# Gathers of two steps issued in one stretch, behind the messages of an odd step

## Chip, core and metric

The kernel runs on one core of a Trainium2 chip. A core has five engines with a queue each: PE (TensorE, matmuls), DVE (VectorE), ACT (ScalarE), POOL (GpSimd) and SP (SyncE, here only for issuing transfers). Each engine takes its instructions in the order of the program and waits on semaphores for the others. The metric is the device time of one execution in microseconds (us).

## What is computed

One layer of a graph network: 6250 nodes with 64 features, 206250 edges sorted by destination, four heads of 16.

```python
Qh = (x @ Wq.T + bq).reshape(n, H, D)
Kh = (x @ Wk.T + bk).reshape(n, H, D)
Vh = (x @ Wv.T + bv).reshape(n, H, D)
Ee = (edge_attr @ We.T + be).reshape(-1, H, D)
score = (Kh[src] * Qh[dst] * (1.0 / np.sqrt(D)) * Ee).sum(-1)
score = jnp.exp(jnp.clip(score, -5.0, 5.0))
msg = Vh[src] * score[..., None]
wV = jax.ops.segment_sum(msg, dst, num_segments=n)
x = _layernorm(x + wV.reshape(n, H * D), axis=-1)
```

## The kernel before

**Node stage.** K and V of all nodes go to a table `kv_tab` in DRAM, one row of 128 numbers a node, and Q to another. While PE computes the pieces of Q (L362, read by ACT at L364), POOL already gathers the rows of the first steps.

**Edge loop.** The edges are cut into 1612 tiles of 128. Eight tiles are a group, and the loop runs over 202 groups; a step is two groups (16 tiles), except for the last eight steps, of one group each. There are 105 steps. Each edge of a tile needs the K and V row of its source node. They come into one of five buffers `kvs[s % KVB]` (KVB = 5), one buffer a step, in two ways:

- 14 of a step's 16 tiles by POOL: `gather_kv` (L446) is one indirect DMA for one tile, 128 rows of 512 bytes. All edges of a tile are gathered at once.
- The last two tiles of steps 3 to 96 by PE: `hots` (L504, DVE) makes one-hot matrices in pieces, `picks` (L515 and L520) multiplies them with the nodes' features, `picked` (L527, L528, ACT) copies the result, `picked_kv` (L531 to L536) makes K and V of it in the PSUM bank `room`, and `place_kv` (L542, ACT) copies them into the buffer. A cycle of picks spreads over four groups, that is two steps, and has a `place_kv` in its second and in its fourth group.

Around it, for each group: `edges` (L561, PE) and `biased` (L567, ACT) make the edge values, `queries` (L573, PE) and `terms` (L580, DVE) multiply them with Q, `turn` (L585, PE) turns the product, `products` (L614 to L619, DVE) multiplies with K and sums to scores, `weigh` (L623, ACT) takes the exponential, and `message` (L630, DVE) multiplies V with it. For each step, `onehot_edges` (L606, DVE) and `widen` (L638, ACT) make a matrix of destinations, `sums` (L643, PE) adds the messages up in `room`, and `add` (L657, DVE) puts them onto the rows of the result. `sums`, `picked_kv`, `place_kv` and `add` share the bank `room`, so they take turns.

**Order.** The order on each engine is the program's. The message of a group is computed in the pass of the next group: in the pass of group g stands `message(g - 1)`. The message of a step's second group is the last reader of that step's buffer. In the pass of a step's first group, behind `message(g - 1)`, the program issues the gathers of the step KVB - 1 = 4 further on, into the buffer that the step before has just left. Each gather waits only for the readers of its own tile: those of the buffer's first eight tiles for the message of the first group, the others for that of the second. Since POOL does nothing else in the loop, its gathers run as far ahead as these waits allow. The products of a step wait for its gathers.

Of the kernel before, what the change touches and what calls it, by code (L numbers as in the profile page):

```python
# [25 lines left out]
NS = len(STEPS)  # L26
# [12 lines left out]
KVB = 5  # L39
# [9 lines left out]
def tiles_of(g):  # L49
    return min(G, T - g * G)  # L50
# [6 lines left out]
def groups_of(s):  # L57
    return range(STEPS[s][0], STEPS[s][0] + STEPS[s][1])
# [18 lines left out]
def picks_in(s):  # L77
    return 0 <= s < 2 * LAST


def is_picked(g, j):

    s = max(s for s in range(NS) if STEPS[s][0] <= g)
    return picks_in(s - AHEAD) and g == groups_of(s)[-1] and j >= G - 2
# [23 lines left out]
def tile_gnn(ctx: ExitStack, tc: tile.TileContext, x, xT, wT, bias, beT, weT, eT, src, src_rows, dst,  # L108
# [17 lines left out]
    def kv_of(g):  # L126

        s = max(s for s in range(NS) if STEPS[s][0] <= g)
        j = (g - STEPS[s][0]) * G
        return kvs[s % KVB][:, j:j + G, :]  # L130
# [39 lines left out]
    def fetch_edges(q):  # L170

        lo, hi = q * LG * G // 2, min((q + 1) * LG * G, T) // 2
        et = loads.tile([P, LG * G // 2, P], F32, name="et")
        nc.sync.dma_start(et[:, :hi - lo, :], eT[:, lo:hi, :])
        for g in range(q * LG, min((q + 1) * LG, NG)):
            ET[g] = et[:, (g % LG) * G // 2:(g % LG + 1) * G // 2, :]

    def fetch_queries(g):

        if g % RG == 0:  # L180
            for i in range(2):
                _, vs = nc.values_load_multi_w_load_instructions(
                    base[i:i + 1, g // 2:(g + RG) // 2], engines=[mybir.EngineType.SP], min_val=0,
                    max_val=N, skip_runtime_bounds_check_because="the least of some destinations")
                for k, v in enumerate(vs):
                    at[g + 2 * k + i] = v
        QW[g] = windows.tile([3 * W, C], BF16, name="qw")
        nc.sync.dma_start(QW[g], q3_tab[bass.ds(at[g], W), :].rearrange("n (i c) -> (n i) c", i=3))

    with tc.tile_pool(name="nodes", bufs=1) as nodes, \  # L190
# [22 lines left out]
        for i in range(NB // CB):  # L213
            s = slice(i * CB * P, (i + 1) * CB * P)
# [229 lines left out]
    def gather_kv(g, j):  # L444
        t = g * G + j
        nc.gpsimd.indirect_dma_start(  # L446
            out=kv_of(g)[:, j, :], out_offset=None, in_=kv_tab[:, :],
            in_offset=bass.IndirectOffsetOnAxis(ap=src_i[:, t:t + 1], axis=0))
# [8 lines left out]
    with tc.If(rv == 0) as branch:  # L457

        with tc.tile_pool(name="work", bufs=2) as work, \
# [21 lines left out]
            def pairs(ap):  # L481

                return ap.rearrange("p (a b) -> p a b", b=2)

            def fetch_sources(m):

                if m < LAST:
                    SRC[m] = work.tile([P, BATCH * P], I32, name="srcs")
                    nc.sync.dma_start(SRC[m], src_rows[m:m + 1, :].to_broadcast([P, BATCH * P]))
# [6 lines left out]
            def pieces(g):  # L496

                return [(g // 4, c) for c in PIECES[g % 4]] if 0 <= g < 4 * LAST else []

            def hots(m, c):  # L500
                lo, hi = CUTS[c], CUTS[c + 1]
                HOT[m, c] = work.tile([P, MOST, BATCH * P], BF16, name="hot", bufs=7)
                shape = [P, hi - lo, BATCH * P // 2, 2]
                nc.vector.tensor_tensor(  # L504
                    HOT[m, c][:, :hi - lo].rearrange("p b (a c) -> p b a c", c=2),
                    pairs(FROM[m])[:, None].to_broadcast(shape),
                    block2[:, lo:hi, None, :].to_broadcast(shape), op=OP.is_equal)
# [33 lines left out]
                n = tiles_in(to)  # L541
                nc.scalar.activation(kvs[to % KVB][:, n - 2:n, :], rooms, AF.Copy)  # L542

            def gather(s):

                for g in groups_of(s):
                    for j in range(tiles_of(g)):
                        if not is_picked(g, j):
                            gather_kv(g, j)

            def fetch_keys(g):

                n = tiles_of(g) * P
                KB[g] = work.tile([3 * W, G * P], BF16, name="kb", bufs=4)
                nc.sync.dma_start(KB[g][:, :n], key_tab[g // 2:g // 2 + 1, g % 2 * G * P:][:, :n]
                                  .to_broadcast([3 * W, n]))
# [54 lines left out]
            def products(g):  # L611
                n = tiles_of(g)
                prod = work.tile([P, G, C], F32, name="prod", bufs=1)
                nc.vector.tensor_mul(prod[:, :n, :], kv_of(g)[:, :n, :C], qe[g % 2][:, :n, :])  # L614
                SCORE[g] = work.tile([P, G, H], F32, name="score", bufs=3)
                score = SCORE[g][:, :n]
                nc.vector.tensor_reduce(score, prod[:, :n, :].rearrange("p g (h d) -> p g h d", h=H),  # L617
                                        axis=AX.X, op=OP.add)
                nc.vector.tensor_scalar(score, score, -5.0, 5.0, op0=OP.max, op1=OP.min)  # L619
# [80 lines left out]
            step_of = {g: s for s in range(NS) for g in groups_of(s)}  # L700
# [18 lines left out]
            biased(2)  # L719
            for mc in pieces(0):  # L720
                hots(*mc)
            for g in range(NG + 1):
                now, before = g < NG, g > 0
                i, m = g % 4, g // 4
                todo, ahead = pieces(g), pieces(g + 1)
                if g % LG == 0 and g + 3 * LG < NG:
                    fetch_edges(g // LG + 3)
                if i == 0 and m:
                    fetch_sources(m + 1)
                if g + 4 < NG:  # L730
                    fetch_queries(g + 4)
                if g + 6 < NG:
                    fetch_keys(g + 6)
                done = ends.get(g - 3)
                if now:
                    products(g)
                for mc in ahead[:1]:
                    hots(*mc)
                if done is not None:
                    add(done)  # L740
                if i == 0 and 0 < m <= LAST:
                    picked(m - 1)
                if i:
                    picks(todo)
                if g + 3 < NG:
                    edges(g + 3)
                if i == 0 and 4 <= g <= 4 * LAST + 2:
                    picked_kv(0)
                if g + 1 < NG:
                    turn(g + 1)  # L750
                if g + 2 < NG:
                    queries(g + 2)
                if g - 2 in ends:
                    sums(ends[g - 2])
                if i == 2 and 4 <= g <= 4 * LAST + 2:
                    picked_kv(1)
                if i == 0:
                    picks(todo)
                if g + 4 < NG:
                    onehot_rows(g + 4)  # L760
                    onehot_rows_rest(g + 4)
                if now:
                    weigh(g)
                else:
                    add(NS - 2)
                if g - 1 in ends:
                    widen(ends[g - 1])
                if g + 3 < NG:
                    biased(g + 3)
                if i == 2 and g < 4 * LAST:  # L770
                    sources(m + 1)
                if i in (1, 3) and 4 <= g <= 4 * LAST + 3:
                    place_kv(m - 1, i // 2)
                if before:
                    message(g - 1)
                if now and g == groups_of(step_of[g])[0] and step_of[g] + KVB - 1 < NS:
                    gather(step_of[g] + KVB - 1)
                if g in ends:
                    s = ends[g]
                    t0 = STEPS[s][0] * G  # L780
                    for t in range(t0, t0 + tiles_in(s)):
                        if t and t % KEYS == 0:
                            keys(t)
                    onehot_edges(s)
                for mc in ahead[1:]:
                    hots(*mc)
                if g + 2 < NG:
                    terms(g + 2)
                if done is not None:

                    while closed < B - 2 and due[closed] <= done + 1:
                        close(closed)
                        spreads(closed)
                        closed += 1
                    if closed in BATCHES and closed > scaled:
                        roots(scaled, closed)
                        scales(scaled, closed)
                        scaled = closed
                    for _ in range(3):
                        if normed < scaled:  # L800
                            norm(normed)
                            normed += 1
# [182 lines left out]
```

## Time and profile before

| | before |
|---|---|
| time, median of 3 runs | 2431.86 us (2424.51 to 2442.23) |
| the profiled execution: time | 2424.42 us |
| the profiled execution: span, mean granted PE clock | 2422.5 us, 0.858 |
| busy: PE, DVE, POOL, ACT | 1953.4, 1479.8, 1352.1, 931.0 us |
| DMA, software queue (the gathers) | 92.37 MB, 14.7% of 16 engines' span |
| DMA, hardware queue (all other) | 133.27 MB, 18.4% |

The span runs from the first to the last instruction of the profiled execution. A line of the timeline gives start and length in us, engine, line of the program, operation, what it writes and reads, and in brackets how long the engine was idle before it and what ended that. "Remote" there is a release that the profile can't put down to an instruction, "issue" one for which it shows no wait. Ends of matmuls are modelled, so an engine that waits for PE can tell more of PE's end than PE's own line. The granted clock is the share of its full clock that PE was given.

### The profile page before, as it was taken

The page shows a single profiled execution, that of the slowest core. Times are in us where ns is not written, and L with a number is a line of the kernel's source. Part 1 is how long each engine was busy: PE and PEld are TensorE (multiplying, and loading weights), DVE is VectorE, ACT ScalarE, POOL GpSimd, SP SyncE. Part 2 cuts the span into 40 slices and gives each one's busy share as a digit, 9 for nine tenths or more (in the row PEclk, how much of TensorE's full clock was granted, in tenths as well). Part 3 has the DMA queues.
Part 4 walks back from the last instruction along what each step waited for, and adds up shares of the span by engine and source line. Part 5 has one row for each costly group of instructions (what it writes and reads, how often), then busy time and mean ns, then how long its engine had stood idle before and what let it go on. Part 6 is the DMA issues. An engine that isn't in the chain of part 4 may idle for free.

```text
span 2422.5 us, 29177 instructions
## 1 busy us (share of the span) xinstructions
PE 1953.4 (81%) x10687; PEld 1157.5 (48%) x10687; DVE 1479.8 (61%) x2314; ACT 931.0 (38%) x1270; POOL 1352.1 (56%) x1434
## 2 busy tenths in 40 slices
PE   4468788788788798888788789788888788878876
PEld 4434444445445455445445445444545445545554
DVE  2356666666666666666666566666666666756654
ACT  1244334344344334424344343343443443443452
POOL 5426555555556565655656555655655655655552
PEclk9998888888889889888888888888879878878975
DMA  4423333233333333333333233333333333332331
GB/s 113 136 78 100 89 95 99 83 102 99 84 102 101 90 97 97 106 86 96 88 101 100 84 100 88 94 102 81 104 104 86 101 102 82 100 98 84 91 103 28
DMA packets 140879, 228.59 MB, mean 94 GB/s; under 512 B 71142, under 2 KB 71592, under 8 KB 140614
## 3 DMA queue, kind: packets, MB, share of 16 engines
q1 hardware_dynamic: 94774, 133.27, 18.4%
q0 software_dynamic: 45568, 92.37, 14.7%
q8 instruction: 86, 1.41, 0.2%
q10 hardware_dynamic: 384, 1.00, 0.2%
q14 instruction: 67, 0.55, 0.1%
HBM read 218.71 MB, written 7.79 MB: 94 GB/s over the span
## 4 chain that ended last, share of the span: by engine, by line
PE 61%; another core or an unknown queue 19%; DVE 8%; ACT 6%; issue 6%; DMA 0%; POOL 0%; DVEq 0%; SPq 0%; ACTq 0%; POOLq 0%
PE pick L515 19%; PE room L643 11%; PE low L520 10%; PE ee L561 7%; PE qe L585 4%; DVE hot L504 3%; PE room L534 3%; PE qq L573 3%; PE room L536 2%; ACT to L598 1%; ACT off L638 1%; ACT eb L567 1%; ACT to L592 1%; PE room L531 1%
## 5 line engine op out<-in xcount | busy, mean ns | idle before, releaser
L446 POOL DMA_INDIRECT kv<-kv_tab,src_i x1392 | 1320.7, 949 | 1017.7 <-DVE msg L630 584.4
L504 DVE TENSOR_TENSOR hot<-from,still 128x2048 bf16<-128x2048 bf16 (+1 forms) x611 | 697.1, 1173 | 113.3 <-PE low L520 92.9
L515 PE MATMUL pick<-hot,parts 128*128 128x512 bf16 x2350 | 567.1, 392 | 7.4 <-issue 6.1
L643 PE MATMUL room<-msg,off 128*128 128x64 f32 x3224 | 440.6, 288 | 133.5 <-issue 127.1
L643 PEld LDWEIGHTS room<-msg,off 128*128 128x128 f32 x3224 | 412.8, 204 | 161.6 <-issue 153.3
L515 PEld LDWEIGHTS <-parts 128*128 128x128 bf16 x2350 | 228.3, 101 | 301.7 <-issue 84.8
L580 DVE TENSOR_TENSOR term<-eb,qq 128x512 f32<-128x512 f32 x202 | 138.2, 684 | 327.2 <-remote 183.9
L561 PE MATMUL ee<-et,we_sb 128*128 128x512 f32 x404 | 268.6, 736 | 80.3 <-issue 50.4
L542 ACT ACTIVATE kv<-room 128x256 f32<-128x256 f32 x94 | 36.0, 383 | 770.4 <-remote 362.2
L567 ACT ACTIVATE eb<-ee,be_col 128x512 f32<-128x512 f32 x202 | 136.3, 675 | 502.7 <-PE ee L561 224.0
L520 PE MATMUL low<-hot,parts 128*64 128x512 bf16 x2350 | 292.8, 384 | 0.6 <-issue 0.4
L657 DVE SCALAR_TENSOR_TENSOR acc<-room,above,acc 128x64 f32<-128x64 f32 x103 | 29.2, 283 | 374.0 <-ACT kv L542 336.6
L598 ACT ACTIVATE to<-to,one_p 126x1024 bf16<-126x1024 bf16 x202 | 231.5, 1146 | 6.6
L592 ACT ACTIVATE to<-kb,minus_row 126x1024 bf16<-126x1024 bf16 x202 | 230.3, 1140 | 0.8 <-DMA kb<-key_tab 0.8
L638 ACT ACTIVATE off<-of 128x2048 f32<-128x2048 bf16 (+2 forms) x105 | 191.8, 1827 | 45.7 <-PE room L643 24.2
L520 PEld LDWEIGHTS <-parts 128*64 128x64 bf16 x2350 | 117.6, 110 | 165.9 <-issue 86.7
L585 PEld LDWEIGHTS qe<-ident,term 128*128 128x128 f32 x806 | 121.7, 166 | 88.7 <-issue 72.1
L531 PE MATMUL room<-bkv_p,ones_b 3*128 3x256 bf16 x94 | 31.4, 334 | 156.3 <-DVE acc L657 152.1
L585 PE MATMUL qe<-ident,term 128*128 128x128 f32 x806 | 147.6, 315 | 4.5 <-DVE term L580 4.5
L561 PEld LDWEIGHTS ee<-et,we_sb 128*128 128x128 f32 x404 | 71.7, 212 | 154.6 <-issue 114.2
L617 DVE TENSOR_REDUCE score<-prod 128x32 f32<-128x512 f32 x202 | 138.3, 685 | 7.0
L614 DVE TENSOR_TENSOR prod<-kv,qe 128x512 f32<-128x512 f32 x202 | 137.5, 681 | 3.8 <-issue 0.2
(122 smaller groups left out, 1274.3 us busy)
## 6 DMA issues: line engine op xcount, KB each, us to landing
et<-in_eT SPq DMA_DIRECT2D x100, 512.0 KB
kb<-key_tab SPq DMA_DIRECT2D x201, 252.0 KB
kv<-kv_tab,src_i POOLq DMA_INDIRECT x1392
srcs<-in_src_rows SPq DMA_DIRECT2D x47, 256.0 KB
qw<-q_tab SPq DMA_DIRECT2D x202, 15.8 KB
kv_tab<-kv_sb SPq DMA_DIRECT2D x5, 640.0 KB
q_tab<-q SPq DMA_DIRECT2D x5, 480.0 KB
acc<-in_x SPq DMA_DIRECT2D x48, 32.0 KB
```

Of the source, the lines that this page charges most:

```text
L446: nc.gpsimd.indirect_dma_start(out=kv_of(g)[:, j, :], out_offset=None, in_=kv_tab[:, :], in_offset=bass.IndirectOffsetOnAxis(ap=src_i[:, t ...
L504: nc.vector.tensor_tensor(HOT[m, c][:, :hi - lo].rearrange("p b (a c) -> p b a c", c=2), pairs(FROM[m])[:, None].to_broadcast(shape), bloc ...
L515: nc.tensor.matmul(hi_mid, parts_flat[:, at:at + 2 * C], hot, start=b == 0, stop=b == NB - 1)
L520: nc.tensor.matmul(low[u * C:(u + 1) * C], parts_flat[:, at:at + C], hot, start=b < 2, stop=b >= NB - 2, skip_group_check=True)
L561: nc.tensor.matmul(ee[:, :n, :], we_sb, ET[g][:, :n, :], start=True, stop=True)
L567: nc.scalar.activation(EB[g][:, :n], ee[:, :n], AF.Identity, bias=be_col)
L585: nc.tensor.transpose(qe[g % 2][:, 2 * u:2 * u + 2, :].rearrange("p j c -> p (j c)"), TERM[g][:, u, :], ident)
L592: nc.scalar.activation(TO[g][:, :n, :], KB.pop(g)[:, :n * P].rearrange("p (j e) -> p j e", j=n), AF.Square, bias=minus_row3[:3 * W])
L598: nc.scalar.activation(TO[g][:, :n, :], TO[g][:, :n, :], AF.Relu, bias=one_p[:3 * W], scale=-1.0)
L617: nc.vector.tensor_reduce(score, prod[:, :n, :].rearrange("p g (h d) -> p g h d", h=H), axis=AX.X, op=OP.add)
L638: nc.scalar.activation(OF[s][:, :n, :], OH.pop(s)[:, :n, :], AF.Copy)
L643: nc.tensor.matmul(pa, OF[s][:, j, :], MSG[s][:, j, :], start=j == 0, stop=j == n - 1)
```

## The change

The gathers of step 4 are issued once ahead of the loop. In the loop, the gathers are issued only in the pass of the first group of an even step s (from step 2 on), for the two steps s + 3 and s + 4 together, behind the message of the last group of the odd step s - 1. The last tile to be gathered of step s + 4 comes first, then all tiles of step s + 3, then the other tiles of step s + 4. Step s + 3 goes into the buffer of step s - 2, step s + 4 into that of step s - 1. The number of gathers and everything on the other engines stay as they are.

```diff
-            def gather(s):
-
-                for g in groups_of(s):
-                    for j in range(tiles_of(g)):
-                        if not is_picked(g, j):
-                            gather_kv(g, j)
+            def tiles_to_gather(s):
+
+                return [(g, j) for g in groups_of(s) for j in range(tiles_of(g)) if not is_picked(g, j)] \
+                    if s < NS else []
+
+            def gathers(s):
+
+                first, then = tiles_to_gather(s), tiles_to_gather(s + 1)
+                for g, j in then[-1:] + first + then[:-1]:
+                    gather_kv(g, j)
...
             for mc in pieces(0):
                 hots(*mc)
+            for g, j in tiles_to_gather(KVB - 1):
+                gather_kv(g, j)
             for g in range(NG + 1):
...
                 if before:
                     message(g - 1)
-                if now and g == groups_of(step_of[g])[0] and step_of[g] + KVB - 1 < NS:
-                    gather(step_of[g] + KVB - 1)
+                if now and g == groups_of(step_of[g])[0] and step_of[g] % 2 == 0 and g:
+                    gathers(step_of[g] + KVB - 2)
```

## The prediction, made before the changed kernel ran

> **What bounds the kernel now.** I read the page first: PE is busy for 81% of the span, POOL for 56%, and the chain that ended last is 61% PE with 19% put down to "another core or an unknown queue". One core runs, so that second share is time the chain could not explain. POOL issues nothing but gathers in the loop:
>
> ```profile
> L446 POOL DMA_INDIRECT kv<-kv_tab,src_i x1392 | 1320.7, 949 | 1017.7 <-DVE msg L630 584.4
> ```
>
> By this line POOL waits 584.4 us for messages, which is the idle time that the change reduces. Idle time matters only where somebody needs the gathers, so next I read the list of waits for who waits in the loop:
>
> ```profile
> POOL kv L446 <- DVE msg L630: 584.4, 139, 38.5
> ...
> ACT kv L542 <- remote: 362.2, 39, 13.2
> DVE acc L657 <- ACT kv L542: 336.6, 80, 7.4
> ```
>
> No VectorE product is listed as waiting for a gather. What stands out is ACT at L542 (`place_kv`), which holds up the add (L657), PE behind it (L531), and the message and POOL behind those. So I read two steps in the middle, PE's busy time window by window (columns: length, then busy us of PE, PEld, DVE, ACT, POOL, granted clock, DMA share, GB/s):
>
> ```profile
> 1166.00:1201.00 35.00, 34.13 (x205) 20.04 (x205) 25.40 (x37) 16.94 (x22) 21.07 (x23) 0.93 0.38 110
> 1201.00:1211.70 10.70, 4.03 (x12) 1.89 (x11) 4.09 (x9) 1.58 (x4) 5.63 (x6) 0.69 0.17 44
> 1211.70:1248.40 36.70, 36.27 (x214) 21.21 (x214) 26.66 (x38) 16.80 (x21) 22.55 (x24) 0.95 0.38 108
> 1248.40:1257.20 8.80, 0.00 (x0) 0.00 (x0) 2.22 (x6) 0.87 (x3) 4.13 (x5) 0.55 0.14 40
> ```
>
> Two steps take 45.6 us (POOL's 14-gather runs start at 1190.70 and 1236.31). PE is full for some 36.5 us of it and then stands nearly still for 9. The timeline of all engines shows what ends that stall:
>
> ```profile
> 1236.31 0.94 POOL L446 DMA_INDIRECT kv<-kv_tab,src_i  x1 [3.42 <-DVE msg L630]
> ...
> 1247.70 0.67 PE L561 MATMUL ee<-et,we_sb 128*128 128x512 f32 x1 [0.16 <-issue]
> ...
> 1252.81 0.94 POOL L446 DMA_INDIRECT kv<-kv_tab,src_i  x1 [0.30 <-issue]
> 1256.33 0.38 ACT L542 ACTIVATE kv<-room 128x256 f32<-128x256 f32 x1 [11.54 <-remote]
> ```
>
> PE's last matmul ends on record at 1248.4. `place_kv` waits for a PE semaphore and gets it at 1256.33, just after a run of 14 gathers, 20.0 us from the run's start: 1.43 us a gather, though POOL issues one each 1.25. I call run length times 1.43 the run's drain. It fits the shorter runs too: six gathers from 1258.09 (drain 1266.7; VectorE's hot, waiting for PE, starts 1266.57), eight from 1268.66 (drain 1280.1; `place_kv` 1280.18).
>
> Is that the gathers, or just PE's work? In one place the order slipped, so that only six gathers stood between two `place_kv`s:
>
> ```profile
> 957.60 0.38 ACT L542 ACTIVATE kv<-room 128x256 f32<-128x256 f32 x1 [7.84 <-remote]
> ...
> 970.63 0.38 ACT L542 ACTIVATE kv<-room 128x256 f32<-128x256 f32 x1 [1.46 <-PE room L643]
> ```
>
> The same half of the period takes 13.0 us there, and 21.8 with 14 gathers in it (1234.55 to 1256.33). So 8.8 us per two steps is the gathers' doing. The nearest row to what the change makes is in the node stage, where 30 gathers stand together while PE feeds ACT with q, one piece each 0.85 us:
>
> ```profile
> 65.47 0.94 POOL L446 DMA_INDIRECT kv<-kv_tab,src_i  x1 [22.85 <-DMA src_i<-in_src]
> ...
> 101.66 0.94 POOL L446 DMA_INDIRECT kv<-kv_tab,src_i  x1 [0.30 <-issue]
> ```
>
> ```profile
> 67.92 0.28 ACT L364 ACTIVATE q<-ps 128x128 bf16<-128x128 f32 x1 [0.41 <-issue]
> ...
> 82.45 0.28 ACT L364 ACTIVATE q<-ps 128x128 bf16<-128x128 f32 x1 [4.00 <-remote]
> 89.44 0.28 ACT L364 ACTIVATE q<-ps 128x128 bf16<-128x128 f32 x1 [6.71 <-remote]
> ...
> 99.24 0.28 ACT L364 ACTIVATE q<-ps 128x128 bf16<-128x128 f32 x1 [9.36 <-remote]
> ...
> 107.69 0.28 ACT L364 ACTIVATE q<-ps 128x128 bf16<-128x128 f32 x1 [1.00 <-remote]
> ```
>
> ```profile
> 50.00:65.00 15.00, 14.39 (x69) 14.14 (x67) 5.13 (x23) 6.66 (x22) 0.00 (x0) 1.00 0.58 218
> 66.00:108.00 42.00, 13.01 (x57) 12.21 (x56) 6.15 (x26) 5.80 (x26) 27.76 (x30) 1.00 0.41 124
> ```
>
> For the first 4 us nothing is lost. Then PE's word comes later and later (4, 7, 9 us apart) until 42.2 us after the first gather (1.41 each), when the rhythm is back. PE is busy for 13.0 of 42 us, at the full granted clock, against 14.4 of 15 before. Every record but PE's own completions stays punctual (DVE follows ACT at once). What is held up inside the chip the trace doesn't say; that it deepens with the run's length is what I use.
>
> **The change part by part.** *Waits removed.* Per two steps POOL stops three times now (runs of 14, 6, 8), and would stop once: message L630 of the odd step's last group releases the last tile of the later step, and the other 27 gathers need nothing later. The 27 are queued behind that wait; their readers are the products six and eight groups on. Six groups are 69 us at 11.4 us a group, the drain of 28 is 28 x 1.43 = 40 us, so no product waits: cost 0, and the saved idle is worth nothing by itself. The earlier step loses two groups of its lead of eight; cover 69 - 40 = 29 us.
>
> *The instructions.* 1392 gathers before and after, each 0.95 us on POOL; SP, ACT and PE queues keep their order. Step 4's 14 gathers already run at 121.2, ahead of the loop: 0.
>
> *The run.* Even steps 2 to 92 issue 28 gathers in one run: 46 runs. How much PE work fits beside one? PE busy in the 14-gather windows was 16.0 of 22 us (1189 to 1211) and 13.0 of 22 (1235 to 1257), in the 30-gather run 13.0 of 42, in the tail's 20-gather run (2355 to 2384) 16.6 of 29 at clock 0.68. It hardly grows with length, so for 28 I take 13 to 16.6, in the middle 14.8. Two steps need 36.5. The run starts 1.8 us after `place_kv` (1256.33 to 1258.09), as now. Period: 1.8 + 40 + (36.5 - 1.8 - 14.8 = 19.9) = 61.7, against 45.6: +16.1, times 46 = 741 us. From both ends: 18 us of work beside the run gives 58.5 (+593), 10 gives 66.5 (+961).
>
> *The stretch behind the drain* has 19.9 us of PE work and no gather. The granted clock was 0.51 from 1249 to 1263 and 1.00 from 1263 to 1281, so a cold start is already inside the 36.5. The Trainium skill (TensorE: Matmul & The Clock Gate, Part 1) has PE fall to half clock after an idle window of about 3.4 us and need as much activity to return; the 0.51 agrees. By that rule each longer stall could add an estimated 1.7 us, 78 us in all (3250); the sum below does without it.
>
> *The tail.* Runs of 8 and a last one of 20 become 16, 16, 16, 12. A longer run loses more, but the 20 goes away: between -14 (the 20-run held three groups for 28.7 us, 2355.1 to 2383.8, where free ones take 4.9 each, as from 2398.7 to 2413.3) and +26 (three 16-runs at the 8.8 of a 14-run). I take 0.
>
> Sum against the profiled execution (2424.4; the shown median is 7 higher): 2424 + 741 = 3165, and with the 7 about **3170 us**.
>
> **The rivals.** *1, faster.* The stall would be order, not starvation: `place_kv` simply lines up with the end of a run because the next run waits for it. Then one wait instead of three leaves POOL's 40.0 us plus one stop of 1.8 as the period: 41.8, -3.8 x 46 = -175, 2255 us. For it: POOL's work with its stops does fill 45.6 (40.0 + 1.8 + 1.8 + about 2). Against it: the 30-gather run, where POOL waits for nobody and ACT still gets PE's word 9 us apart. It decides if PE does its 36.5 us beside a 40 us run; it needs over 34 there and did 13. The Trainium skill (SBUF — State Buffer, Who interferes with whom) says that PE and ACT never wait on anyone and that only VectorE and GpSimd share a port; it speaks for this rival, and PE's 0.00 us busy from 1248.4 to 1257.2 speaks against it.
>
> *2, no change.* Each gather costs PE the same wherever it stands: 45.6 stays, 2430 us. Against it: 8.8 us lost to 14 gathers where six lost nothing.
>
> *3, slower, but less.* A 28-run loses only twice what a 14-run does: 36.5 + 17.6 = 54.1, +8.5 x 46 = 391, 2820 us. For it: the main loop's PE work (picks of 14 matmuls at a time) asks for fewer signals than the q stage. Against it: 13.0 of 42.
>
> *That the run breaks*, since gathers of the earlier step find a wait of their own, falls under 2; the releasing messages lie four groups back, so I see none.
>
> **How the numbers follow.** Forecast: 0.75; its own range is 3010 (2431 + 593 - 14) to 3420 (2431 + 961 + 26). Rival 3: 0.08. Rival 1: 0.13. Rival 2: 0.04. The range runs from 2750, which takes in rival 3, to 3420; it leaves out rivals 1 and 2 (0.17) and little above. About 1% is what this measurement can tell from no change. Faster 0.13, same 0.03 (most of rival 2), slower 0.84.
>
> **What would show it.** POOL: runs of 28, one wait for L630 per two steps, some 50 waits instead of 139. ACT's L542: the wait ahead of the drain grows from 8-13 to some 20 us. PE: windows of over 15 us almost empty in each period, then about 20 us full; granted clock below 0.858. Period near 62 us. I am wrong if PE stays busy through a run's second half, or if a product waits for a gather.

## The result, and the profile after

| four runs each | before | after |
|---|---|---|
| median | 2432.16 us (2424.51 to 2442.23) | 3218.43 us (3214.84 to 3222.48) |
| span of the profiled execution, granted clock | 2422.5 us, 0.858 | 3216.5 us, 0.770 |
| PE busy | 1953.4 us (81%) | 2058.0 us (64%) |
| ratio | | 1.323, 95% interval 1.318 to 1.328 |

The changed kernel is a third slower. The record names no chip for this comparison; its two kernels are taken as run on one. From L543 on its lines lie four further down than before's (L567 is now L571, L580 is L584, L630 is L634). The costliest group of POOL on the page after:

```profile
L446 POOL DMA_INDIRECT kv<-kv_tab,src_i x1392 | 1317.8, 947 | 1812.5 <-DVE msg L634 1359.7
```

The list of waits after (us in total, times, longest):

```profile
POOL kv L446 <- DVE msg L634: 1359.7, 49, 57.5
ACT eb L571 <- remote: 1328.4, 43, 35.1
DVE term L584 <- remote: 1078.3, 43, 29.3
...
PE room L647 <- issue: 918.3, 725, 3.2
...
ACT kv L542 <- remote: 76.7, 5, 16.5
```

POOL stops 49 times instead of 139, so the gathers do stand together. It waits 775 us more for messages all the same: they come late, because everything does. The waits that the profile can't put down to an instruction have moved: `place_kv` (L542) had 362.2 us of them and has 76.7, while `biased` on ACT and `terms` on DVE now have 43 each, some 31 and 25 us long. Both read what PE makes. PE itself stands ahead of its matmuls of `sums` (L647) for 918.3 us in 725 pieces, 127.1 in 165 before, and the profile shows nothing that it waits for there ("issue").

One period of the loop, window by window (length, then busy us of PE, PEld, DVE, ACT, POOL, granted clock, DMA share, GB/s). The run of 28 gathers starts at 1948.53:

```profile
1948.50:1958.50 10.00, 10.00 (x64) 4.60 (x62) 8.26 (x13) 6.62 (x8) 7.56 (x8) 1.00 0.61 183
1958.50:1968.50 10.00, 4.23 (x17) 2.07 (x13) 1.77 (x2) 0.00 (x0) 7.54 (x8) 0.84 0.22 54
1968.50:1978.50 10.00, 1.32 (x5) 1.72 (x6) 0.00 (x0) 0.00 (x0) 7.55 (x8) 0.50 0.21 52
1978.50:1988.20 9.70, 2.00 (x7) 1.65 (x7) 0.00 (x0) 0.04 (x1) 3.77 (x4) 0.50 0.14 34
1988.20:2007.10 18.90, 18.90 (x92) 10.42 (x93) 13.90 (x20) 9.42 (x12) 0.00 (x0) 0.79 0.19 57
```

For 10 us PE is full, for 30 it hardly works, and when the run is over it is full again. The timeline of the same stretch:

```profile
1948.53 0.94 POOL L446 DMA_INDIRECT kv<-kv_tab,src_i  x1 [27.81 <-DVE msg L634]
...
1978.89 0.26 PE L647 MATMUL room<-msg,off 128*128 128x64 f32 x1 [1.84 <-issue]
1980.99 0.27 PE L647 MATMUL room<-msg,off 128*128 128x64 f32 x1 [1.84 <-issue]
1983.79 0.26 PE L647 MATMUL room<-msg,off 128*128 128x64 f32 x1 [2.53 <-issue]
1985.19 0.26 PE L647 MATMUL room<-msg,off 128*128 128x64 f32 x1 [1.14 <-issue]
...
1988.16 0.69 ACT L571 ACTIVATE eb<-ee,be_col 128x512 f32<-128x512 f32 x1 [32.98 <-remote]
1988.33 0.69 DVE L584 TENSOR_TENSOR term<-eb,qq 128x512 f32<-128x512 f32 x1 [25.77 <-remote]
```

Two things are to be seen. PE's matmuls in the stall start 2.10, 2.80 and 1.40 us apart, multiples of 0.70: over the whole execution, 270, 192 and 171 gaps between starts lie at 0.64 to 0.76, 1.35 to 1.46 and 2.05 to 2.15 us. And ACT gets PE's word at 1988.16, 39.6 us from the run's start, or 1.415 us a gather: the 1.43 that the prediction took from before. In 40 of the 45 intervals between runs of 28 ACT's longest wait ends 39.4 to 39.9 us behind the run's first gather; in the other five ACT is released once in between, and again after 39.8 to 39.9 us.

### The profile page after: what moved, and what is told of

It reads as the page before. It is cut to its first block, busy times and chain, and to the rows that moved or that the text cites. A ratio compares the mean times of both kernels' runs of the same rounds, so it can differ in the third digit from the quotient of the medians.

```text
span 3216.5 us, 28986 instructions
## 1 busy us (share of the span) xinstructions
PE 2058.0 (64%) x10687; PEld 1256.6 (39%) x10687; DVE 1474.6 (46%) x2314; ACT 938.1 (29%) x1270; POOL 1349.3 (42%) x1434
## 3 DMA queue, kind: packets, MB, share of 16 engines
q1 hardware_dynamic: 94774, 133.27, 13.9%
q0 software_dynamic: 45568, 92.37, 11.5%
q8 instruction: 86, 1.41, 0.2%
## 4 chain that ended last, share of the span: by engine, by line
PE 50%; issue 31%; DVE 11%; another core or an unknown queue 5%; ACT 1%; POOL 1%; DMA 0%; DVEq 0%; SPq 0%; ACTq 0%
PE pick L515 16%; PE room L647 14%; PE low L520 7%; DVE hot L504 4%; PE ee L565 4%; PE qe L589 2%; PE qq L577 2%; PE room L534 1%; DVE score L621 1%; DVE prod L618 1%; POOL kv L446 1%; DVE term L584 1%; DVE of L610 1%; PE room L536 1%
## 5 line engine op out<-in xcount | busy, mean ns | idle before, releaser
L647 PE MATMUL room<-msg,off 128*128 128x64 f32 x3224 | 593.9, 316 | 925.2 <-issue 918.3
L647 PEld LDWEIGHTS room<-msg,off 128*128 128x128 f32 x3224 | 560.4, 242 | 976.9 <-issue 969.1
L584 DVE TENSOR_TENSOR term<-eb,qq 128x512 f32<-128x512 f32 x202 | 137.6, 681 | 1430.3 <-remote 1078.3
L515 PE MATMUL pick<-hot,parts 128*128 128x512 bf16 x2350 | 619.8, 419 | 24.9 <-issue 23.8
L571 ACT ACTIVATE eb<-ee,be_col 128x512 f32<-128x512 f32 x202 | 137.5, 680 | 1682.4 <-remote 1328.4
L515 PEld LDWEIGHTS <-parts 128*128 128x128 bf16 x2350 | 246.2, 109 | 354.7 <-issue 163.5
L565 PE MATMUL ee<-et,we_sb 128*128 128x512 f32 x404 | 231.9, 656 | 43.3 <-ACT eb L571 26.8
L542 ACT ACTIVATE kv<-room 128x256 f32<-128x256 f32 x94 | 36.1, 384 | 385.0 <-PE room L647 289.2
L589 PE MATMUL qe<-ident,term 128*128 128x128 f32 x806 | 132.5, 281 | 21.4 <-issue 19.2
L589 PEld LDWEIGHTS qe<-ident,term 128*128 128x128 f32 x806 | 104.0, 146 | 107.3 <-issue 101.0
L634 DVE TENSOR_TENSOR msg<-kv,score 128x512 f32<-128x512 f32 x202 | 137.7, 682 | 0.0
L610 DVE TENSOR_TENSOR of<-still,key 128x2048 bf16<-128x2048 bf16 (+2 forms) x105 | 123.3, 1174 | 0.4
L577 PE MATMUL qq<-to,qw 126*64 126x512 bf16 x404 | 95.2, 415 | 34.1 <-issue 27.0
```

Source lines behind the costliest of these rows:

```text
L515: nc.tensor.matmul(hi_mid, parts_flat[:, at:at + 2 * C], hot, start=b == 0, stop=b == NB - 1)
L565: nc.tensor.matmul(ee[:, :n, :], we_sb, ET[g][:, :n, :], start=True, stop=True)
L584: nc.vector.tensor_mul(TERM[g][:, :n], EB.pop(g)[:, :n], qq[:, :n])
L589: nc.tensor.transpose(qe[g % 2][:, 2 * u:2 * u + 2, :].rearrange("p j c -> p (j c)"), TERM[g][:, u, :], ident)
L647: nc.tensor.matmul(pa, OF[s][:, j, :], MSG[s][:, j, :], start=j == 0, stop=j == n - 1)
```

## The experiments

The theory was the prediction's: gathers that POOL issues 1.25 us apart hold PE up, the more the longer the run. Within it two readings differ. One (A) is a backlog: POOL issues faster than something behind it gets done (1.25 against 1.42 us), so slower issue would cure it. The other (B) is the length of a run as such, whatever its pace. Rivals were the order of the gathers, and the bytes that they move.

Most experiments ran on other chips than the first comparison, and that turned out to matter more than any edit. Each group of runs had runs of the kernel before beside it:

| chip | before | experiments |
|---|---|---|
| the one above | 2432.16 us | before and after |
| a second, at two times | 1853.44 and 1856.28 us | e1 to e4; e8 to e10 |
| a third | 1858.55 us | e5 to e7 |
| a fourth | 1856.60 us | e11 |
| one more, or the first again | 2440.37 us | e12 |

The expectations of e1 to e4 were written for a chip like the first. All four times came out below every range that they give, and the later ones name a range for each kind of chip. That it is the chip, and not something else that changes from one group of runs to the next, is a reading: only the second chip was used at two times, and it took some 1855 us at both.

### The same two kernels on another chip (e5, e6)

No edit: after and before, as they are.

> The changed kernel itself, unaltered, on the chip of this call. In the first call the kernel before took 1853 us in place of 2432, and variants of the changed kernel 1846 to 1857, so the starvation was not there at all. Theory A, made narrower: PE starves beside gathers only in some surroundings (a chip, or the place on it that the run gets); where the kernel before takes about 1853 us, the changed one takes the same within 1% (1835 to 1875), with PE busy over 90%. Where the kernel before takes 2432 us, the changed one takes 3218 again. Rival: the one run of 28 costs time everywhere (1.32 times the kernel before, 2450 us where that takes 1853).

> The kernel before, for its profile on this chip. Where it takes 1853 us: no wait of ACT at L542 over 8 us, PE busy over 90% of the span, and in the node stage's run of 30 gathers no pieces of q that come 4 to 10 us apart. Where it takes 2432 us: the profile of before again.

After took 1874.87 us against 1858.55 for before: ratio 1.0098 (1.0075 to 1.0122). The waits of the changed kernel there:

```profile
ACT eb L571 <- PE ee L565: 408.9, 141, 7.7
...
DVE prod L618 <- DMA kv<-kv_tab,src_i: 72.6, 25, 9.6
...
POOL kv L446 <- DVE msg L634: 36.2, 4, 34.5
```

The stall is gone from both kernels. ACT's longest wait for PE is 7.7 us in after, the gaps of 1.35 to 1.46 and 2.05 to 2.15 us between PE's starts number 1 and 2 instead of 192 and 171, and PE is busy for 93% of the span (94% in before). In before (e6) POOL's 1348 gathers of the loop form one unbroken run at the same 1.25 us each (median), 48 times as long as a run of 28, and in after (e5) they have one stop, of 1.1 us behind the first 28; PE works beside them. In the node stage of e6, too, the pieces of q come 0.85 us apart beside the gathers. So neither the edit nor a long run of gathers stalls PE by itself; something that differs between these executions and the first has to come in.

### Pacing the gathers (e1, e7, e9, e4)

After, and for e4 before, with a filler on POOL behind each gather of the loop (224 columns, in e4 128):

```diff
...
                     gather_kv(g, j)
+                    nc.gpsimd.iota(pace_i, pattern=[[1, 224]], base=0, channel_multiplier=0)
```

> The changed kernel, with one small POOL instruction (an iota of 224 columns into a scratch tile, 0.32 us in the node stage) behind each gather of the loop's runs. Nothing else differs, and the run of 28 becomes longer in time. Theory A (backlog): POOL issues a gather each 1.25 us, they drain one each 1.43 us, and PE starves while a backlog stands. With about 1.55 us from gather to gather no backlog arises: PE goes on through the run, no ACT wait of over 10 us, the period is POOL's own, 28 x 1.55 + 1.8 = 45.2 us in place of 62.6, time about 2420 us (2330 to 2520). Theory B (length): what starves PE is the run's length, so many gathers without a pause. Then the stall stays or grows with the longer run: 3220 us or more.

> The kernel before, with an iota of 128 columns (0.22 us) behind each gather of the loop: about 1.46 us from gather to gather, just over the drain of 1.43. Theory A: the 8.8 us that a 14-run takes from PE go, POOL's 28 x 1.46 = 40.9 us and its stops remain: period 42.7 (one stop of 1.8) to 46.5 (stops as before, 5.6), 2290 to 2465 us, with ACT's waits at L542 under 8 us. Theory B: the runs are as long or longer, so the stalls stay and POOL's extra 28 x 0.21 = 5.9 us add to the period: 2430 to 2700 us.

> The changed kernel with an iota of 224 columns behind each gather, as in the first call, where it took 2143 us and POOL was the bound (81% of its chain). On a chip without starvation 2143 again. On a chip with it, theory A (backlog) has 2330 to 2520, theory B (length of the run) 3220 or more.

> The changed kernel with an iota of 224 columns behind each gather of the loop, which holds POOL back so that gathers are issued some 1.6 to 1.7 us apart instead of 1.25. Where before takes some 1855 us: POOL is the bound, some 2145 us as twice measured, no stall of PE over 7 us. Where before takes some 2430 us: if PE is held up because gathers are issued faster (1.25 us) than they are done (1.43 us) and the backlog grows with the run, pacing takes the backlog away, the wait of the biased values (33 us) falls below 8 us and the time is 2140 to 2300 us; if any long run of gathers starves PE whatever its pace, PE stays starved through a run of 28 x 1.65 = 46 us and the time is over 3200 us.

After paced took 2142.60, 2147.42 and 2149.01 us, before paced 2005.08. e1 has a ratio to before of 1.156 (1.151 to 1.161), e4 one of 1.082 (1.076 to 1.089). The chain that ended last in e1, by engine and by line:

```profile
POOL 81%; issue 11%; DVE 3%; PE 3%; DMA 1%; ACT 1%; SPq 0%; POOLq 0%; DVEq 0%; ACTq 0%
POOL kv L447 60%; POOL pace_i L555 21%; DVE hot L505 1%; PE ps L363 1%; PE room L649 1%; PE pv L397 1%; PE ps L333 0%; DMA rows_i<-in_dst_rows 0%; DVE score L623 0%; DMA kb<-key_tab 0%; DMA kv<-kv_tab,src_i 0%; PE ps L408 0%; DVE prod L620 0%; ACT to L604 0%; DMA w_sb<-in_bias 0%
```

Where PE isn't held up, POOL is close to the bound already (in e6 it issues the loop's gathers without a break from 114.3 to 1830.7 us), and both fillers on it lengthened the kernel. A and B weren't told apart: there was no stall to cure. Neither this edit nor the two that follow was ever run on a chip that has one.

### The natural order (e2, e8)

```diff
-                for g, j in then[-1:] + first + then[:-1]:
+                for g, j in first + then:
```

> The changed kernel with one part undone: the tiles in their natural order (step s + 3, then step s + 4), so that the run is no longer held for one message. The 14 gathers of step s + 3 find their buffer long free and run on behind the 6 last of the run before; the 8 first and 6 last of step s + 4 wait for messages of their own. Theory A: runs of 20 and 8. Beside 20 gathers (drain 28.6 us) some 15 us of PE work fit, beside 8 (11.4 us) some 9.5, the other 12 of the 36.5 stand free: period 52 us, 2424 + 46 x 6.6 = 2730 us (2600 to 2900). If the pairing of two steps itself were the cost, and not how long the run is: 3220 us as in the changed kernel.

> The changed kernel, but the 28 gathers of an even step in their natural order (the earlier step's 14 first, then the later step's), so that POOL waits only for a message of the step before and not first for the last one. Two kinds of chip have been seen, so each theory has two numbers. Where before takes some 1855 us and POOL is never idle: if the 1% that the change costs there comes from the one early wait for the odd step's last message (its lead over the products is shorter), this order gives it back, 1853 to 1861 us, and products wait for gathers under 20 us in all; if it comes from the merging of two steps as such, it stays at 1871 to 1881 us with some 70 us of waits for gathers. Where before takes some 2430 us: the starvation theory has the same runs of 28 in either order, period near 62 us, 3150 to 3250 us; if it was the early wait that lined POOL's run up against PE, under 2700 us.

1857.23 and 1856.50 us; the second, over 10 runs, has a ratio to before of 1.0005 (0.999 to 1.002). So the 1% goes with the order, the one line. Three profiles show where it sits. The first gather of the loop's long run, after (e5), before (e6) and in natural order (e8):

```profile
132.81 0.95 POOL L446 DMA_INDIRECT kv<-kv_tab,src_i  x1 [34.51 <-DVE msg L634]
```

```profile
114.28 0.94 POOL L446 DMA_INDIRECT kv<-kv_tab,src_i  x1 [16.45 <-DVE msg L630]
```

```profile
108.81 0.94 POOL L446 DMA_INDIRECT kv<-kv_tab,src_i  x1 [10.80 <-DVE msg L634]
```

And the list of waits of e8:

```profile
DVE prod L618 <- DMA kv<-kv_tab,src_i: 11.4, 3, 5.0
```

From there POOL needs 1713.4, 1716.4 and 1717.1 us to its last gather in the three of them. With the last tile first, POOL waits long once (34.5 of 36.2 us), ahead of the loop's first run, for the message of the odd step, and starts 18.5 us later than before; 16.3 us is the difference of the medians. From there it is busy almost without a break and ends 15.5 us later than before, so the products wait for gathers 25 times (72.6 us) instead of 3 (11.4 us). In natural order it starts 5.5 us earlier than before and gains nothing clear of the noise by it: the chain that ended last is 57% PE and 14% POOL there, where in e5 it is 40% POOL and 29% PE. The two ratios come from two chips, each against before's runs on its own.

### Half of each gather (e3, e10)

Each gather fetches 64 of its 128 rows; half of the gathered K and V rows are left out. The buffers are set to zero once at the start, so zeros stand there.

```diff
...
-            out=kv_of(g)[:, j, :], out_offset=None, in_=kv_tab[:, :],
-            in_offset=bass.IndirectOffsetOnAxis(ap=src_i[:, t:t + 1], axis=0))
+            out=kv_of(g)[:P // 2, j, :], out_offset=None, in_=kv_tab[:, :],
+            in_offset=bass.IndirectOffsetOnAxis(ap=src_i[:P // 2, t:t + 1], axis=0))
```

> The changed kernel with each gather of the loop and of the first steps cut to 64 of its 128 rows; it leaves out half of the gathered rows, whose places in the buffers hold zeros. Same number of gathers, same order, same waits. Theory A with a drain that goes by rows: 0.7 us a gather, under the 1.25 us of POOL's issue (or the issue shrinks as well), so no backlog and no stall: period between PE's 36.5 and 42 us, 2000 to 2260 us. With a drain that goes by gathers, whatever their size, or theory B: the stall stays, 3100 to 3250 us.

> The changed kernel with every gather fetching 64 of its 128 rows, so half of the gathered K and V rows are left out (zeros stand there); the issue on POOL is unchanged. Where before takes some 1855 us: PE-bound, 1840 to 1860 us, as measured once. Where before takes some 2430 us: if what holds PE up is the number of rows (packets) that a gather moves, half of them drain faster than they are issued, and the time is below 2100 us; if it is the number of gather instructions or POOL's own work for them, the time stays above 3000 us.

1846.19 and 1844.80 us, one run each, with PE busy for 95% of the span in both: 7 and 11 us under before's medians, while single runs of before go down to 1849.51 and 1848.79, so little can be read from that. Again no chip with a stall, so whether a gather's bytes or the gather itself holds PE up stays untried.

### Slow gathers made on purpose (e11, e12)

One copy inside DRAM for each two steps, so that gathers share the DMA engines with it, in after (e11) and, at the same steps, in before (e12):

```diff
...
+                    if step_of[g] + KVB - 2 < NS:
+                        k = step_of[g] // 2
+                        nc.scalar.dma_start(spare[k % 4], eT[:, k * 8:k * 8 + 128, :])
```

> The changed kernel with one more transfer for each two steps: ACT issues a copy of 8.4 MB inside DRAM behind the gathers, 386 MB in all, so that the gathers have to share the DMA engines and are done more slowly than POOL issues them (1.25 us); nothing waits for the copy but the fifth one behind it. It tries to bring about on any chip what the long runs of gathers do where before takes some 2430 us. If PE is held up there because gathers are done more slowly than they are issued, the copies do the same where before takes some 1855 us: ACT's biased values wait for PE over 20 us at a time, PE's windows of 10 us inside a run fall below 3 us busy, and the time is over 2300 us. If slow gathers alone do not hold PE up, what comes late is their data: the waits of VectorE's products for the gathers grow from 72.6 us to several hundred, no other engine is held up first, and the time is 1900 to 2300 us, or 1875 to 1890 us if the DMA engines have room for both.

> The kernel before with the same copies inside DRAM as in the last experiment (8.4 MB for each two steps, at the same places of ACT's order). It asks whether gathers that are issued in three stretches per two steps, with a lead of eight groups for each step, bear slow gathers better than one stretch of 28. Where before takes some 1855 us: if the DMA engines' work sets the period (gathers, copies and loads share them), both kernels come out alike, 2650 to 2850 us; if the later gathers of the changed kernel's earlier step cost part of it, as they do the 1% without copies, this one is faster by the DMA waits that they spare, 2400 to 2650 us. Where before takes some 2430 us, gathers and copies share the engines there as well, and nothing under 2650 us is expected.

There were 50 copies of 8.4 MB, not 46: the queue moved 420.43 MB. e11, on a chip without stalls, took 2747.28 us (one run), over the 2300 that was to part the two theories. What it waits for has to decide:

```profile
DVE prod L619 <- DMA kv<-kv_tab,src_i: 1028.0, 116, 21.2
POOL kv L447 <- DMA kv<-kv_tab,src_i: 943.9, 221, 7.5
...
ACT eb L572 <- PE ee L566: 185.9, 56, 7.7
```

The products wait for gathers, 1028 us in all (loads of keys come late too, with 513.0 us on ACT); ACT's longest wait for PE is as long as without copies; of PE's gaps at 1.4 and 2.1 us there are 8. Here slow gathers deliver their data late and don't bring about the stall. The first theory's bound on the time was met for the other theory's reason. The test is weaker than it was meant to be: POOL waited for its own gathers 221 times, so in much of the run the gathers were issued slowly as well, and the chip is one on which nothing else brings the stall about either.

e12 came to a chip where before takes 2440.37 us, so its 2940.90 us (one run) can't be set against e11, and the question of its expectation stays open; it is over 2650, as expected for such a chip. But its profile has two kinds of stretches side by side. First, while a copy keeps the DMA engines full and POOL has to wait for its own gathers; then a run of 39 gathers with no copy beside it:

```profile
1350.00:1370.00 20.00, 20.00 (x132) 12.67 (x131) 16.82 (x27) 9.45 (x13) 4.10 (x5) 1.00 0.89 291
1390.00:1405.00 15.00, 15.00 (x100) 9.09 (x99) 10.76 (x20) 5.78 (x7) 1.89 (x2) 1.00 0.89 282
1446.30:1466.30 20.00, 14.77 (x77) 8.64 (x77) 11.87 (x18) 8.39 (x10) 15.38 (x16) 0.80 0.46 123
1466.30:1501.20 34.90, 0.86 (x1) 0.00 (x0) 0.00 (x0) 0.00 (x0) 21.84 (x24) 0.50 0.17 45
```

```profile
1354.85 0.95 POOL L447 DMA_INDIRECT kv<-kv_tab,src_i  x1 [4.53 <-DMA kv<-kv_tab,src_i]
1361.43 0.94 POOL L447 DMA_INDIRECT kv<-kv_tab,src_i  x1 [5.64 <-DMA kv<-kv_tab,src_i]
...
1446.34 0.95 POOL L447 DMA_INDIRECT kv<-kv_tab,src_i  x1 [3.09 <-DMA kv<-kv_tab,src_i]
...
1494.21 0.94 POOL L447 DMA_INDIRECT kv<-kv_tab,src_i  x1 [0.30 <-issue]
...
1501.24 0.38 ACT L543 ACTIVATE kv<-room 128x256 f32<-128x256 f32 x1 [42.84 <-remote]
```

With gathers some 6.5 us apart, PE is full, though the DMA engines are busy for 89% of the time. With 39 gathers 1.25 us apart, PE does 0.86 us of work in the last 34.9, with the DMA engines at 17%, and its word comes 54.9 us from the run's start: 1.41 a gather, as with 28, and close to the 1.43 with 14. Over the loop, windows of 10 us with seven or more gathers have 5.9 us of PE work (80 of them); those with at most three gathers and a copy have 9.1 (67). So on a chip that stalls it is gathers in close succession that go with the stall, not the load on the DMA engines; gathers held apart go without it. And the order of the gathers isn't needed for it: this run of 39, like those of 14 and of 30, stands in before's order and has the same delay a gather. The slow stretches speak for A. They are no proof of it, since the copies did the pacing and no stretch holds a long run at a slow pace without them.

## Why the prediction was right, point by point

- **POOL's waits.** Runs of 28 and some 50 waits were forecast; 46 such runs in the loop, then 16, 16 and 28 (two of the forecast tail's runs joined), and 49 waits. That the saved waits are worth nothing held: no product waits for a gather there.
- **The drain of 40 us.** 28 x 1.43 was forecast; 39.5 measured (median of 45 periods). The rule that a run of n gathers holds PE's word back for 1.42 n held from 14 to 39 gathers. The word "drain" was loose, though: the last packet of the run at 1948.53 lands at 1984.48, 3.7 us before PE's word, and that of the run of 39 at 1496.51, 4.7 us before (1.25 us for the 14 at 1236.31 in before). The gathers' data are not what takes 1.42 us each: in the run at 1948.53 they land 2.2 us behind the start of their gather at its end as in its middle (1962.28 to 1964.53, 1982.26 to 1984.48). If there is a backlog, it isn't one of data.
- **PE's work beside the run.** 14.8 us taken, from 13 to 16.6; 17.6 measured, above that range. It does saturate: 17.6 of 39.5 us, 10 of it in the first 10.
- **PE's work behind it.** From the end of the stall to the next run pass 23.4 us (median), of which PE works 23.0; 19.9 + 1.8 = 21.7 was forecast. Two steps so take 17.6 + 23.0 = 40.6 us of PE, not 36.5. The 36.5 was too small for before already: it counts one full stretch alone, but the other period in the same windows has 34.13 + 4.03 = 38.2, and over before's loop (166 to 2290 us) PE is busy for 1780.8 of 2124 us, 38.2 in 45.6. Only 2.4 of the 4.1 us came with the change. Of the 4.1, 2.8 are done beside the run. So two terms were too small and partly made up for each other; that the period came to 62.6 us (mean) on a forecast of 61.7 is in part luck. Times 46, the 17.0 us over before's 45.6 make 782 of the 794 us between the spans.
- **The clock.** "A cold start is already inside the 36.5" was the weak sentence: the granted clock is 0.50 from 1968 to 1988 and 0.79 in the 19 us of work behind, and 0.77 on the whole. PE's 2.4 us more in two steps fit that, though no run here shows that the clock is all of it. The Trainium skill (TensorE: Matmul & The Clock Gate, Part 1) has PE fall to half clock after an idle window and need as much activity to return, which the prediction made an estimated 3250 us; the trace agrees on the half clock (0.50), and its 3218 us lie between that estimate and the 3170 without it.
- **Which wait grows.** This step failed: not L542 grew to some 20 us but `biased` (33 us) and `terms` (26). The run now begins behind the `place_kv` of the cycle's fourth group, as before's runs of six did, and not behind that of the second group, as the runs of 14 did; so others of PE's readers stand in the stall. The size, too, was too small: with PE full for the first 10 us of 39.5, some 30 are left.
- **The rivals.** The first, faster by PE and POOL side by side, fell in this comparison: PE did 17.6 us beside the run, not 36.5. Half of it is what the chips of 1855 us do: PE works there beside an unbroken run. The changed kernel isn't faster there either: POOL issues without a break in before's loop (e6), so there is no idle time to remove. The second fell with the period of 62.6 us. The third (a run of 28 loses twice what a run of 14 does) fell with PE's idle time, 22.0 us in a period against 45.6 - 38.2 = 7.4 before: three times as much. The Trainium skill's sentence that PE and ACT never wait on anyone (SBUF — State Buffer, Who interferes with whom) agrees with those chips. On the first, PE's 2.00 of 9.70 us in the last window of the run speaks against taking it as a forecast, though the trace doesn't say that the SBUF is where PE is held.

What the prediction could not know, and what stays open, is why the same kernel stalls on some chips and not on others: it did in the first comparison and in e12 (whether these are one chip isn't on record), and not on three others. There the forecast of 3170 us would have been far off, so that it came right is also due to where the kernel ran. The profiles of both kinds show the same pace of gathers within a run (median 1.25 us), and for before the same bytes (92.37 MB of gathers, 133.27 MB of the rest).

## What to carry to other kernels

Before a run of indirect gathers is made longer, look at what PE does beside the longest run that the profile has, even in another stage: a stall of 42 us behind 30 gathers in the node stage foretold the 39.5 behind 28 in the loop. An idle engine is worth nothing if what it is to run faster takes the critical engine's time; and where that engine runs without a break, as POOL does on the other chips, the thing to look for is what delays its first instruction. Compare kernels on one chip only: before alone takes some 1855 or 2435 us, and an edit that costs 1% on the one costs 32% on the other.

## What the runs showed of the hardware

- In the first comparison and in e12, PE's matmuls beside long runs of gathers issued 1.25 us apart start in steps of 0.70 us, half of the 1.41 that each gather adds to PE's delay, or for a time not at all (0.00 us busy from 1248.4 to 1257.2 in before); in e5 and e6, at the same pace of gathers, they go on. What PE and the gathers share is not shown.
- A DMA engine share of 0.89 beside PE's 20.00 of 20 us is what the Trainium skill says of DMA and engines (SBUF — State Buffer, Who interferes with whom: DMA itself doesn't contend with a compute engine); this trace (e12) agrees.
- While copies of 8.4 MB were under way, POOL waited up to 7.6 us at a time for its own gathers in flight: 943.9 us in e11, 755.2 in e12. Without the copies such waits are 0.6 us at most.
